# A selective-scan kernel: products written over the drive, six drive buffers, all state copies on ScalarE, and unit 12 of first passes on GpSimd

## The chip, the cores and the metric

The kernel runs on one core of one Trainium2 chip. A core has five engines that each work through their own queue in order: TensorE (PE), VectorE (DVE), ScalarE (ACT), GpSimd (POOL) and SyncE (SP, which issues the DMAs here). TensorE writes PSUM; the other memory is SBUF. The metric is the time of one launch on the device in microseconds (us); lower is better.

## The reference

Two layers run on an input of 8 images of 64 channels and 128x128 pixels in float32. The first makes nine weights per pixel with a small convolution and a softmax, and filters each channel with them. The second is a block around a bidirectional state-space model ("Mamba"), with a convolution, a gated branch and a feed-forward net behind it. What matters here is the selective scan, which runs for each image, for two layers and in two directions over the 16,384 pixels as a sequence:

```python
def selective_scan(u, dt, A, Bm, Cm, D, z):
    dt = jax.nn.softplus(dt)
    dA = jnp.exp(jnp.einsum('bdl,dn->bldn', dt, A))
    dBu = jnp.einsum('bdl,bnl,bdl->bldn', dt, Bm, u)
    ...
    _, hs = jax.lax.associative_scan(comb, (dA, dBu), axis=1)
    y = jnp.einsum('bldn,bnl->bdl', hs, Cm) + D[None, :, None] * u
    return y * jax.nn.silu(z)
```

With 128 channels d and 16 states n, each position has 2,048 recurrences h = dA * h + dBu. The kernel calls dA the decay `w`, dBu the drive `bu`, and hs * Cm the product.

## The kernel before, in words

**Chunks and units.** A scan over 16,384 positions is cut into 16 chunks of T = 1024. One image has four scans ("passes") one after the other: layer 0 forward (pass 0) and backward (pass 1), layer 1 backward (pass 2) and forward (pass 3). Passes 0 and 2 are the first of their layer; passes 1 and 3 have `second` set, add the result of the first, and apply the gate and the output projection. So there are 8 x 4 x 16 = 512 chunks. In a chunk the 2,048 recurrences are 16 units u of 128 partitions, and two units make a pair k = u // 2, whose states j and channel group gp the table `PAIRS` gives.

**One unit.** `decay` (L1124, ACT) writes w = exp(dt * A) into one of two PSUM tiles. `drive` (L1116, POOL) writes the drive of a whole pair, 128x2048, into a `bu` tile in SBUF. `scan` (L1142 or L1144 by direction, DVE) runs the recurrence over 1024 positions from the state of the chunk before. `product` multiplies by Cm. It has two forms, and `on_pool(u)` chooses:
- on POOL, units 0, 2, 6, 8, 10 and 14: the scan writes into `hs` in SBUF, POOL copies the last column into `state` (L1161) and multiplies `hs` in place (L1162);
- on DVE, all odd units and units 4 and 12: the scan writes over w in PSUM, DVE multiplies w into `hs` (L1165), and ACT copies the last column into `state` (L1166).

A unit with an even number that falls just behind a GELU of the feed-forward net also goes to DVE. `collect` (L1181, PE) sums a pair's products over the states with matmuls against `sel_y`. The pair tile `hs` has four buffers of 128x2048, and so has `bu`.

**Feeding a chunk.** Two chunks ahead, matmuls and activations make x, dt, B and C for it (with a SiLU at step 11 and a softplus at step 18 of that chunk, each with loads of activation tables). `dtx` (L1072, POOL) multiplies dt by x, `store_du` and its neighbours write to DRAM, and `load_channels` and `load_states` (L1083, L1094) load the tiles `dup`, `dtp`, `bp` and `cp` back, spread over partitions.

**Other work beside the scans.** Per image and 16 times each: `Front` (the first layer and three norms) of the next image, during passes 2 and 3; `Mix` (convolutions and the product with the branch), late in pass 3 and in pass 0 of the next image; `Ffn` (the feed-forward net), in the rest of pass 0 and pass 1. Their matmuls, `tmp` tiles and multiplications run on the same engines. Behind the last scan comes a tail with the last image's feed-forward net.

**What sets the order.** Nothing is reordered by a scheduler. Each operation is put down by `at(time, phase, fn)`, where `time` is a step (one unit is one step, a chunk starts at step b) and `phase` orders the operations within a step: FEED, SCAN, MID, PROD, EXP, DECAY, REST. The queues are filled in that order; within one step and phase, in the order of the calls. For the units of a chunk:

```python
for k in range(U // 2):
    at(b + 2 * k - 5, REST, self.drive, k)
    at(b + 2 * k + 3 + (k % 4 == 0), REST, self.collect, k)
for u in range(U):
    at(b + u - 2, EXP, self.decay, u)
    at(b + u, SCAN, self.scan, u)
    at(b + u + self.on_pool(u), FEED if self.on_pool(u) else PROD, self.product, u)
```

POOL's queue thus alternates: the product of an even unit u at step u + 1, then at the same step the drive of the pair that begins six steps after u. Two steps earlier or later there is another such pair of instructions; `dtx` stands at step 5 of the chunk before its own (b - 11).

Of the kernel before, what the change touches and what calls it, by code (L numbers as in the profile page):

```python
# [8 lines left out]
F32 = mybir.dt.float32  # L9
BF16 = mybir.dt.bfloat16  # L10
AF = mybir.ActivationFunctionType
ALU = mybir.AluOpType
# [3 lines left out]
P = 128  # L16
# [14 lines left out]
T = 1024  # L31
# [3 lines left out]
U = G * G  # L35
PW = W + 2
FEED, SCAN, MID, PROD, EXP, DECAY, REST = range(7)
# [18 lines left out]
def kernel(ctx: ExitStack, tc: tile.TileContext, a: dict, out: bass.AP):  # L56
# [6 lines left out]
    nc = tc.nc  # L63
# [128 lines left out]
    with tc.tile_pool(name="wspill", bufs=1) as fp, tc.tile_pool(name="wprep", bufs=2) as pp, \  # L192
            tc.tile_pool(name="wps", bufs=4, space=PSUM) as pps:
        with tc.manual_schedule():
# [49 lines left out]
            fw = a["L1_conv_ffn_in_w"].rearrange("o c i j -> o (c i j)")  # L244
# [21 lines left out]
            for k in range(9):  # L266
                i, j = divmod(k, 3)
# [130 lines left out]
    def at(time, phase, fn, *args):  # L398
        steps.setdefault((time, phase), []).append((fn, args))
# [386 lines left out]
    class Ffn:  # L786
# [6 lines left out]
        def load(self, h):  # L793
            if not self.alone:
                self.win[h] = window(xn_img, "fw")
            else:
                if h == 0:
                    self.fw = wk.tile([P, 2, T], F32, tag="bu", name="fw", bufs=4)
                self.win[h] = self.fw[:, h, 0 : (ROWS + 2) * PW].rearrange("p (r w) -> p r w", w=PW)
            load_shifted(self.win[h], xn_img, self.c, h)  # L800

# [42 lines left out]
                    )  # L844

        def before_taps_out(self):
            self.pre = wk.tile([P, 2, T], F32, tag="hs", name="f1", bufs=4)
            for i, bank in enumerate(self.banks):
                lo = 3 * PW * (i % 2)
                nc.scalar.copy(self.pre[:, i // 2, lo : lo + 3 * PW], bank[:, 0 : 3 * PW])  # L850
# [107 lines left out]
    class Chunk:  # L958


        def __init__(self, i):
            self.b, self.l, self.d, self.t, self.second = order[i]
            self.i, self.t0 = i, U * i
            self.first = i % NT == 0
            self.pairs = PAIRS[i % 2]
            r, last = self.t0 % IMAGE, self.b == B - 1
            self.beside_front = (
                FRONT_AT - FRONT_STEP <= r < FRONT_AT + NCH * FRONT_STEP + 16 and not last
            ) or self.t0 < FIRST_FRONT_AT + NCH * FRONT_STEP + 16
            self.prev = None  # L970
            self.bus, self.hss, self.ws = {}, {}, {}
            self.dup, self.dtp, self.bp, self.cp, self.yv = {}, {}, {}, {}, {}
            self.norm = Norm()

# [127 lines left out]
        def on_pool(self, u):  # L1102


            if u % 2 or u % 8 == 4 or self.t0 + u - 1 in gelu_times:
                return False
            return True

        def over_pair(self, what, k):
            j = self.pairs[k][0]  # L1110
# [1 line left out]
            return src.rearrange("p (o t) -> p o t", o=1).to_broadcast([P, 2, T])  # L1112

        def drive(self, k):
            bu = wk.tile([P, 2, T], F32, tag="bu", name="bu", bufs=4)
            nc.gpsimd.tensor_tensor(bu, self.dup[self.pairs[k][1]], self.over_pair("bp", k), ALU.mult)  # L1116
            self.bus[k] = bu

# [10 lines left out]
        def scan(self, u):  # L1129
            k, i = divmod(u, 2)  # L1130
            if u == 0:
                if self.first:
                    self.state = wk.tile([P, U], F32, tag="state", name="state")
                    nc.vector.memset(self.state, 0.0)
                else:
                    self.state = self.prev.state
            if i == 0:
                self.hss[k] = wk.tile([P, 2, T], F32, tag="hs", name="hs", bufs=4)
            w, hs, bu, s0 = self.ws.pop(u), self.hss[k][:, i, :], self.bus[k][:, i, :], self.column(u)
            to = hs if self.on_pool(u) else w  # L1140
            if self.d == 0:
                nc.vector.tensor_tensor_scan(to, w, bu, s0, ALU.mult, ALU.add)  # L1142
            else:
                nc.vector.tensor_tensor_scan(to[:, ::-1], w[:, ::-1], bu[:, ::-1], s0, ALU.mult, ALU.add)  # L1144
            if not self.on_pool(u):
                self.ws[u] = w

        def column(self, u):
            (j, gp), i = self.pairs[u // 2], u % 2
# [5 lines left out]

        def product(self, u):
            k, i = divmod(u, 2)
            j, hs = self.pairs[k][0], self.hss[k][:, i, :]
            c = self.cp[j // 2][:, j % 2, :]
            if self.on_pool(u):  # L1160
                nc.gpsimd.tensor_copy(self.column(u), self.last(hs))  # L1161
                nc.gpsimd.tensor_tensor(hs, hs, c, ALU.mult)  # L1162
            else:
                w = self.ws.pop(u)
                nc.vector.tensor_tensor(hs, w, c, ALU.mult)  # L1165
                nc.scalar.copy(self.column(u), self.last(w))  # L1166

        def collect(self, k):

            hs, gp = self.hss.pop(k), self.pairs[k][1]  # L1170
            if k % 4 == 0:
                self.y = py.tile([P, N], F32, tag="y", name="y")
                for h, s in enumerate(halves):
                    nc.tensor.matmul(  # L1174
                        self.y[C * h : C * h + C, :], dskip[:, self.l, self.d, C * gp : C * gp + C], self.xc[:, s],
                        start=True, stop=False,
                    )
            for h, s in enumerate(halves):
# [63 lines left out]
        def plan(self):  # L1242
# [23 lines left out]
            at(b - 16, DECAY, self.bc_out)  # L1266
            at(b - 14, REST, self.store_bc)
            at(b - 13, REST, self.store_dt)
            at(b - 11, FEED, self.dtx)
            at(b - 10, REST, self.store_du)  # L1270
            j0 = self.pairs[0][0] // 2
            at(b - 10, REST, self.load_states, "bp", j0)
            at(b - 8, REST, self.load_channels, "dup", 0)
            at(b - 6, REST, self.load_channels, "dtp", 0)
            at(b - 5, REST, self.load_states, "bp", 1 - j0)
            at(b - 4, REST, self.load_states, "cp", j0)
            at(b - 3, REST, self.load_channels, "dup", 1)
# [85 lines left out]
```

## Time and profile before

Three runs took 28,833.31, 28,854.13 and 28,859.38 us; the median is 28,854.13. The profiled execution took 28,835.68 us, with a span of 28,833.6 us from the first to the last instruction.

| | per chunk, or in all |
|---|---|
| set-up before the first scan, tail behind the last | 481.8 us, 443.1 us |
| decay on ACT, 8,192 instructions | 1,119 ns each |
| scan on DVE, 8,192 | 2,343 ns each |
| product on DVE, 5,232 | 1,222 ns each |
| product on POOL, 2,960 | 2,352 ns each |
| drive on POOL, 4,096 (two units each) | 4,534 ns each |
| dt times x on POOL, 512 | 2,361 ns each |
| state copy on POOL, 2,960; on ACT, 5,232 | 187 ns; 158 ns each |

How to read it: a chunk takes about 54 us in passes 0 to 2 and 57 us in pass 3, as the starts of the scans of unit 0 show. Durations of neighbours on one engine overlap by some tens of ns in these records, so that the distance from start to start of back-to-back instructions is what an instruction really takes of its engine. An idle time is put down to the instruction behind it, with what ended it ("releaser"). The share of a whole run hides that the four passes differ, so passes are looked at one by one below. For image 4 of 0 to 7 they run from 14,465 to 15,329, to 16,190, to 17,051 and to 17,960 us.

### The profile page before, as it was taken

The page shows a single profiled execution, that of the slowest core. Times are in us where ns is not written, and L with a number is a line of the kernel's source. Part 1 is how long each engine was busy: PE and PEld are TensorE (multiplying, and loading weights), DVE is VectorE, ACT ScalarE, POOL GpSimd, SP SyncE. Part 2 cuts the span into 40 slices and gives each one's busy share as a digit, 9 for nine tenths or more (in the row PEclk, how much of TensorE's full clock was granted, in tenths as well). Part 3 has the DMA queues.
Part 4 walks back from the last instruction along what each step waited for, and adds up shares of the span by engine and source line. Part 5 has one row for each costly group of instructions (what it writes and reads, how often), then busy time and mean ns, then how long its engine had stood idle before and what let it go on. Part 6 is the DMA issues. An engine that isn't in the chain of part 4 may idle for free. (4 is left out here: it accounts for less than half of the span.)

```text
span 28833.6 us, 311734 instructions
## 1 busy us (share of the span) xinstructions
PE 22961.3 (80%) x97708; PEld 7243.9 (25%) x97708; DVE 27012.9 (94%) x17438; ACT 18542.2 (64%) x26170; POOL 27201.8 (94%) x11052
## 2 busy tenths in 40 slices
PE   6666888878788787887878788787887878878578
PEld 3111222223222232222322222222222222222123
DVE  5999999999999999999999999999999999999997
ACT  3666666666666666666666666666666666666663
POOL 3999999999999999999999999999999999999993
PEclk7777888988899888998989889898888988889779
DMA  5776777777777678776777767777777777777574
GB/s 133 226 243 219 237 252 241 247 225 240 255 240 247 226 237 259 238 244 226 243 252 242 239 229 245 248 247 234 233 249 240 252 229 235 251 240 250 203 249 140
DMA packets 2592273, 6762.77 MB, mean 235 GB/s; under 512 B 431270, under 2 KB 736822, under 8 KB 2589462
## 3 DMA queue, kind: packets, MB, share of 16 engines
q1 hardware_dynamic: 2590614, 6742.83, 71.8%
q8 instruction: 775, 12.70, 0.2%
q14 instruction: 884, 7.24, 0.1%
HBM read 5509.49 MB, written 1265.19 MB: 235 GB/s over the span
## 5 line engine op out<-in xcount | busy, mean ns | idle before, releaser
L1116 POOL TENSOR_TENSOR bu<-dup,bp 128x2048 f32<-128x2048 f32 x4096 | 18545.3, 4534 | 9.9 <-DMA dup<-du_dram 2.4
L1124 ACT ACTIVATE w<-dtp,a_neg 128x1024 f32<-128x1024 f32 x8192 | 9159.5, 1119 | 1642.2 <-DVE hs L1144 695.4
L1162 POOL TENSOR_TENSOR hs<-hs,cp 128x1024 f32<-128x1024 f32 x2960 | 6963.1, 2352 | 243.3 <-DMA cp<-bc_dram 5.1
L1165 DVE TENSOR_TENSOR hs<-w,cp 128x1024 f32<-128x1024 f32 x5232 | 6391.3, 1222 | 273.1 <-DMA cp<-bc_dram 96.1
L1144 DVE TENSOR_TENSOR_SCAN w<-w,state,bu 128x1024 f32<-128x1024 f32 x2651 | 6212.3, 2343 | 113.9 <-ACT w L1124 85.6
L1142 DVE TENSOR_TENSOR_SCAN w<-w,state,bu 128x1024 f32<-128x1024 f32 x2581 | 6049.4, 2344 | 173.0 <-ACT w L1124 144.4
L1181 PE MATMUL y<-hs,sel_y 128*32 128x512 f32 x32768 | 4983.5, 688 | 694.4 <-POOL hs L1162 693.6
L1166 ACT COPY state<-w 128x1 f32<-128x1 f32 x5232 | 828.2, 158 | 5460.1 <-DVE hs L1165 5401.8
L1142 DVE TENSOR_TENSOR_SCAN hs<-w,state,bu 128x1024 f32<-128x1024 f32 x1515 | 3548.9, 2343 | 173.4 <-ACT state L1166 71.9
L1144 DVE TENSOR_TENSOR_SCAN hs<-w,state,bu 128x1024 f32<-128x1024 f32 x1445 | 3384.8, 2342 | 151.2 <-ACT state L1166 65.9
L991 PE MATMUL xp<-hn,wx 128*128 128x512 f32 x4096 | 2332.5, 698 | 757.3 <-ACT xc L997 320.9
L822 PE MATMUL fp<-fw,bgw 128*128 128x512 f32 (+1 forms) x5760 | 2196.5, 625 | 242.7 <-DMA fw<-xn_dram 230.9
L1174 PE MATMUL y<-xc,dskip 128*64 128x512 f32 x4096 | 1442.1, 790 | 1123.1 <-ACT yv L1198 972.4
L1033 PE MATMUL dp<-xc,wdt 128*128 128x512 f32 x2048 | 1336.5, 739 | 581.5 <-ACT dt L1040 274.3
L1181 PEld LDWEIGHTS y<-hs,sel_y 128*32 128x32 f32 x32768 | 714.7, 115 | 4242.9 <-issue 2328.2
L68 ACT ACT_TABLE_LOAD x1137 | 1458.8, 1283 | 20.8 <-PEq L1352 0.7
L997 ACT ACTIVATE xc<-xp,cbias 128x512 f32<-128x512 f32 x1024 | 697.6, 681 | 1160.2 <-PE xp L991 1157.0
L828 PE MATMUL fp<-fw,bgw 64*128 64x512 f32 (+1 forms) x5760 | 1381.4, 606 | 0.0
L991 PEld LDWEIGHTS xp<-hn,wx 128*128 128x128 f32 x4096 | 795.2, 212 | 2161.9 <-issue 861.6
L595 PE MATMUL acc<-t,ident 128*128 128x512 f32 x2160 | 1330.5, 703 | 0.0
L580 PE MATMUL wb<-wt,sel_k 65*128 65x512 bf16 x1152 | 509.3, 448 | 919.5 <-DVE t L584 810.3
L1072 POOL TENSOR_TENSOR du<-dt,xc 128x1024 f32<-128x1024 f32 x512 | 1208.7, 2361 | 30.1 <-ACT dt L1046 30.1
(211 smaller groups left out, 24922.6 us busy)
## 6 DMA issues: line engine op xcount, KB each, us to landing
bp<-bc_dram SPq DMA_DIRECT2D x4096, 256.0 KB, 4.0
dup<-du_dram SPq DMA_DIRECT2D x4096, 256.0 KB, 5.2
dtp<-dt_dram SPq DMA_DIRECT2D x4096, 256.0 KB, 5.1
cp<-bc_dram SPq DMA_DIRECT2D x4096, 256.0 KB, 4.8
hn<-hn_dram SPq DMA_DIRECT2D x1024, 256.5 KB, 4.4
dt_dram<-dt SPq DMA_DIRECT2D x512, 512.0 KB, 3.0
du_dram<-du SPq DMA_DIRECT2D x512, 512.0 KB, 2.6
yf_dram<-yv SPq DMA_DIRECT2D x512, 256.0 KB, 4.5
```

Source lines behind the costliest of these rows:

```text
L68: nc.scalar.preload_act_table_set("natural_log_exp_and_others")
L822: nc.tensor.matmul(o, wpair[:, i, g, m], self.win[h][:, i : i + ROWS, 0:W], start=(i == 0), stop=False)
L828: nc.tensor.matmul(o, wlast[rows, i, g, m], self.win[h][rows, i : i + ROWS, lo : W + lo], start=False, stop=(i == 2),)
L991: nc.tensor.matmul(self.xp[h], wx[:, self.l, self.d, i, :], self.hn2[:, s.start + 2 * i : s.stop + 2 * i], start=(i == 0), stop=(i == 1),)
L1116: nc.gpsimd.tensor_tensor(bu, self.dup[self.pairs[k][1]], self.over_pair("bp", k), ALU.mult)
L1124: nc.scalar.activation(w, self.dtp[gp][:, i, :], AF.Exp, scale=a_neg[:, self.l, self.d, g, j : j + 1])
L1142: nc.vector.tensor_tensor_scan(to, w, bu, s0, ALU.mult, ALU.add)
L1144: nc.vector.tensor_tensor_scan(to[:, ::-1], w[:, ::-1], bu[:, ::-1], s0, ALU.mult, ALU.add)
L1162: nc.gpsimd.tensor_tensor(hs, hs, c, ALU.mult)
L1165: nc.vector.tensor_tensor(hs, w, c, ALU.mult)
L1174: nc.tensor.matmul(self.y[C * h : C * h + C, :], dskip[:, self.l, self.d, C * gp : C * gp + C], self.xc[:, s], start=True, stop=False,)
L1181: nc.tensor.matmul(self.y[lo : lo + 32, :], sel_y, hs[:, i, s], start=False, stop=(k % 4 == 3))
```

## The change

- A product is written over its unit's half of the drive tile `bu` instead of into `hs`, on POOL and on DVE alike, and `collect` reads `bu`. The drive tile lives until its `collect`, and `bu` has six buffers instead of four. `hs` is now a tile of one unit (128x1024, four buffers), allocated only for units whose product is on POOL. Two tiles of the last image's feed-forward net (`fw`, `f1`) take `bu` buffers.
- `keep` copies the last column into `state` on ACT for every unit. For a unit on DVE it stands where the ACT copy stood; for a unit on POOL it stands in phase EXP of the step behind the unit, after that step's decay. POOL makes no state copies any more.
- `on_pool` keeps unit 4 on DVE and gives unit 12 to POOL in chunks of first passes.
- `drive` is put down one step earlier, and with it `dtx`, `store_du`, the loads of `bp` and the first load of `dup`.

```diff
         def before_taps_out(self):
-            self.pre = wk.tile([P, 2, T], F32, tag="hs", name="f1", bufs=4)
+            self.pre = wk.tile([P, 2, T], F32, tag="bu", name="f1", bufs=6)
...
-            if u % 2 or u % 8 == 4 or self.t0 + u - 1 in gelu_times:
+            if u % 2 or u == 4 or self.t0 + u - 1 in gelu_times:
                 return False
-            return True
+            return u != 12 or not self.second
...
         def drive(self, k):
-            bu = wk.tile([P, 2, T], F32, tag="bu", name="bu", bufs=4)
+            bu = wk.tile([P, 2, T], F32, tag="bu", name="bu", bufs=6)
             nc.gpsimd.tensor_tensor(bu, self.dup[self.pairs[k][1]], self.over_pair("bp", k), ALU.mult)
...
-            if i == 0:
-                self.hss[k] = wk.tile([P, 2, T], F32, tag="hs", name="hs", bufs=4)
-            w, hs, bu, s0 = self.ws.pop(u), self.hss[k][:, i, :], self.bus[k][:, i, :], self.column(u)
-            to = hs if self.on_pool(u) else w
+            w, bu, s0 = self.ws.pop(u), self.bus[k][:, i, :], self.column(u)
+            to = wk.tile([P, T], F32, tag="hs", name="hs", bufs=4) if self.on_pool(u) else w
+            self.hs[u] = to
...
         def product(self, u):
             k, i = divmod(u, 2)
-            j, hs = self.pairs[k][0], self.hss[k][:, i, :]
-            c = self.cp[j // 2][:, j % 2, :]
-            if self.on_pool(u):
-                nc.gpsimd.tensor_copy(self.column(u), self.last(hs))
-                nc.gpsimd.tensor_tensor(hs, hs, c, ALU.mult)
-            else:
-                w = self.ws.pop(u)
-                nc.vector.tensor_tensor(hs, w, c, ALU.mult)
-                nc.scalar.copy(self.column(u), self.last(w))
+            engine = nc.gpsimd if self.on_pool(u) else nc.vector
+            engine.tensor_tensor(
+                self.bus[k][:, i, :], self.hs[u], self.cp[self.pairs[k][0] // 2][:, self.pairs[k][0] % 2, :], ALU.mult
+            )
+
+        def keep(self, u):
+            nc.scalar.copy(self.column(u), self.last(self.hs.pop(u)))
...
-            hs, gp = self.hss.pop(k), self.pairs[k][1]
+            hs, gp = self.bus.pop(k), self.pairs[k][1]
...
-            at(b - 11, FEED, self.dtx)
-            at(b - 10, REST, self.store_du)
+            at(b - 12, FEED, self.dtx)
+            at(b - 11, REST, self.store_du)
             j0 = self.pairs[0][0] // 2
-            at(b - 10, REST, self.load_states, "bp", j0)
-            at(b - 8, REST, self.load_channels, "dup", 0)
+            at(b - 11, REST, self.load_states, "bp", j0)
+            at(b - 9, REST, self.load_channels, "dup", 0)
             at(b - 6, REST, self.load_channels, "dtp", 0)
-            at(b - 5, REST, self.load_states, "bp", 1 - j0)
+            at(b - 6, REST, self.load_states, "bp", 1 - j0)
...
-                at(b + 2 * k - 5, REST, self.drive, k)
+                at(b + 2 * k - 6, REST, self.drive, k)
...
+            for u in range(U):
+                at(b + u + self.on_pool(u), EXP if self.on_pool(u) else PROD, self.keep, u)
```

More of the change, by code (lines that the diff above doesn't have):

```diff
@@ L797, in load @@
                 if h == 0:
-                    self.fw = wk.tile([P, 2, T], F32, tag="bu", name="fw", bufs=4)
+                    self.fw = wk.tile([P, 2, T], F32, tag="bu", name="fw", bufs=6)
                 self.win[h] = self.fw[:, h, 0 : (ROWS + 2) * PW].rearrange("p (r w) -> p r w", w=PW)
@@ L970, in __init__ @@
             self.prev = None
-            self.bus, self.hss, self.ws = {}, {}, {}
+            self.bus, self.hs, self.ws = {}, {}, {}
             self.dup, self.dtp, self.bp, self.cp, self.yv = {}, {}, {}, {}, {}
@@ L1144, in scan @@
                 nc.vector.tensor_tensor_scan(to[:, ::-1], w[:, ::-1], bu[:, ::-1], s0, ALU.mult, ALU.add)
-            if not self.on_pool(u):
-                self.ws[u] = w
         def column(self, u):
```

## The prediction

> **What bounds the kernel now.** I read the page first. In its 40 slices both DVE and POOL are at 9 nearly everywhere, so the whole does not say which of the two it is.
>
> ```profile
> DVE  5999999999999999999999999999999999999997
> POOL 3999999999999999999999999999999999999993
> ```
>
> So I cut one image (image 4) into its four passes, by the starts of the scans of unit 0, and read the busy time of each engine per pass, in the order pass 0, 1, 2, 3.
>
> ```profile
> core 0: us, PE busy (x) PEld busy (x) DVE busy (x) ACT busy (x) POOL busy (x), PEclk, DMA share, GB/s
> 14465.00:15329.00 864.00, 677.53 (x2834) 181.64 (x2832) 803.20 (x460) 551.22 (x747) 856.56 (x345) 0.87 0.76 246
> 15329.00:16190.00 861.00, 761.90 (x3166) 236.23 (x3164) 832.36 (x506) 584.84 (x795) 832.11 (x318) 0.96 0.74 249
> 16190.00:17051.00 861.00, 656.80 (x2750) 204.79 (x2748) 833.33 (x541) 565.07 (x804) 850.31 (x357) 0.83 0.70 227
> 17051.00:17960.00 909.00, 758.30 (x3533) 273.38 (x3531) 869.97 (x610) 614.93 (x922) 856.19 (x360) 0.90 0.74 242
> ```
>
> In pass 0 POOL is busy 856.56 of 864 us and DVE idles 61 us; in pass 2 POOL leaves 10.7 us and DVE 27.7. In passes 1 and 3 POOL leaves 29 and 53 us, DVE 29 and 39. The groups and waits of POOL say what its rest is: first pass 0 (two groups), then the one large wait of passes 1 and 3.
>
> ```profile
> L1162 POOL TENSOR_TENSOR hs<-hs,cp 128x1024 f32<-128x1024 f32 x93 | 218.8, 2352 | 7.4
> L1161 POOL COPY state<-hs 128x1 f32<-128x1 f32 x93 | 17.4, 187 | 0.0
> ...
> POOL state L1161 <- DVE hs L1144: 22.0, 13, 3.6
> ...
> POOL state L1161 <- DVE hs L1142: 24.9, 19, 3.8
> ```
>
> In pass 0 the only idle time of POOL is 7.4 us, the 80 ns between a state copy and its product (93 times). It waits for nobody: **passes 0 and 2 last as long as POOL's queue.** In passes 1 and 3 POOL waits for scans: there DVE sets the pace. What DVE itself waits for there, in pass 1 (first line) and pass 3 (last two):
>
> ```profile
> DVE w L1144 <- ACT w L1124: 9.9, 6, 2.7
> ...
> DVE t L584 <- PE wb L580: 19.2, 12, 3.0
> DVE hs L1142 <- ACT state L1166: 6.3, 10, 0.9
> ```
>
> Decays that come late from ACT, and matmuls of the front; POOL's drives are not among them. Summing the gaps of the whole trace by pass, and following each releaser back along its engine until DVE or a DMA is met, 0.04 us per chunk of DVE's 1.63 us in pass 1, and 0.02 of 2.49 in pass 3, lead through POOL.
>
> **The change part by part.** *The state copies leave POOL.* Durations overlap, so I take distances from start to start. The timeline of POOL in pass 0:
>
> ```profile
> 14599.96 4.54 POOL L1116 TENSOR_TENSOR bu<-dup,bp 128x2048 f32<-128x2048 f32 x1
> 14604.44 0.18 POOL L1161 COPY state<-hs 128x1 f32<-128x1 f32 x1
> 14604.70 2.35 POOL L1162 TENSOR_TENSOR hs<-hs,cp 128x1024 f32<-128x1024 f32 x1
> 14607.01 4.53 POOL L1116 TENSOR_TENSOR bu<-dup,bp 128x2048 f32<-128x2048 f32 x1
> ```
>
> Drive to copy is 4.48 us, copy to product 0.26, product to drive 2.31. Over the trace the medians are 4.474, 0.265 and 2.310, and drive to drive, with no copy between, is 4.494 (551 cases). A copy thus costs 4.474 + 0.265 - 4.494 = 0.245 us. Passes 0 and 2 have 747 + 754 = 1,501 copies (six a chunk, less 21 and 14 that a GELU sends to DVE): 1,501 x 0.245 = **-368 us**. By the busy row alone (187 ns) it would be -281; the 80 ns gap belongs to the copy and goes with it, so I take the spacing and keep both ends. The Trainium skill (Perfetto Trace Analysis, "GPSIMD Engine Instruction") likewise says that a GpSimd span is unreliable and that start-to-start spacing is to be used; here the two readings differ by 87 us, and the trace's own gaps favour the spacing.
>
> *Unit 12 goes to POOL in first passes.* 256 chunks, none of them behind a GELU, each one product more between two drives: 256 x 2.312 (mean from a product's start to the next drive) = **+592 us** on POOL. Writing into `bu` instead of in place makes three separate tiles, as `dt` times x has, which takes the same (2,361 ns, next start after 2.315). DVE loses 256 x 1.222 = 313 us in the passes where it idles anyway: worth nothing, the cover being POOL's full queue. Were POOL not full there, this would be the gain.
>
> So per first-pass chunk POOL gets 2.31 - 1.44 = 0.87 us longer; in all +224 us, with no idle time on POOL to take it.
>
> *In second passes* POOL loses 1,459 x 0.245 = 357 us of work. It was waiting for scans there, so I cost this at nothing; what is late next is the scan, as now. Products end 0.26 us earlier, which PE's `collect` could use: PE waits for POOL's products 0.84 us per chunk in pass 1 and 0.37 in pass 3. If all of that came back to DVE it would be (0.84 + 0.37) x 128 = 155 us; by the followed waits it is 0.06 x 128 = 8. I take 0 and keep -155 as the low end.
>
> *Drives one step earlier, and six buffers.* On POOL's queue the drive of pair m + 3 now stands before the product of unit 2m instead of behind it; `dtx` keeps its place behind the product of unit 2. The new wait is that a drive waits for the `collect` of six drives before. Today a drive starts at least 3.9 us (pass 0) and 3.4 us (pass 2) behind that point, with medians of 16 and 15, and in POOL's order it moves up by one product, 2.6 us at most: no wait. In pass 1 it moves up by as much as a pair's time (6.7 us) and a tenth of the drives have under 3.7, so waits of some 3 us will be seen; queued behind such a drive is the product of the scan just running. POOL's 1.1 us of waiting per chunk and the 1.3 us of copies removed cover these; without that cover they would cost about 0.6 us a chunk, 80 us.
>
> *The earlier DMAs.* `dup` is needed sooner: from the store of `du` to the first drive of the next chunk POOL has 21.06 us of work now and 18.1 then (three drives and three products with copies now, three drives and two products without then). The store, the `bp` load (which waits for drive 5, directly behind `dtx` as before) and the `dup` load on SP keep their spacing. Today `dup` lands 6.9 us (pass 0) and 6.6 us (pass 2) before that drive in the median, 4.2 and 3.2 at the tenth percentile. Taking 2.96 us from each landing that the trace records leaves none short in pass 0 and 0.12 us a chunk in pass 2: **+15 us**; bounds 0 and, with three times that in both passes, 77.
>
> *All copies on ACT.* 2,960 more at 0.159 us and a gap of 0.033, 0.19 us each, 562 us in all on an ACT that idles 17 to 19 us in each chunk, mostly for DVE's products. Two questions. Does such a copy wait? ACT's copies now start when the DVE product ends, not the scan (5,401.8 us of idle time, "ACT state<-w" behind "DVE hs L1165"), though both only read w; if the new ones waited for POOL's product in the same way, ACT would stand still 2 to 10 us after many scans. But w lies in PSUM and `hs` in SBUF. The Trainium skill (PSUM — Partial Sum Buffer, "PSUM bank collisions raise a hardware error") says that two engines may not even both read a bank at once and must be kept apart by semaphores; by that rule only copies from PSUM wait. The trace has no ACT read of `hs`; the scan alone writes it, and the copy needs only that, so I take no wait and keep the other as a rival. Second, where is ACT's own work the path? Behind the SiLU. In pass 1, ACT:
>
> ```profile
> 15534.31 0.16 ACT L1166 COPY state<-w 128x1 f32<-128x1 f32 x1 [0.28 <-DVE hs L1165]
> ...
> 15540.44 1.12 ACT L1124 ACTIVATE w<-dtp,a_neg 128x1024 f32<-128x1024 f32 x1
> ```
>
> and DVE, which waits at unit 14:
>
> ```profile
> 15541.66 2.35 DVE L1144 TENSOR_TENSOR_SCAN hs<-w,state,bu 128x1024 f32<-128x1024 f32 x1 [0.34 <-ACT state L1166]
> ```
>
> From the copy behind product 11 (15534.31) to the end of decay 14 (15541.56) ACT works without a pause, and scan 14 waits 0.34 us for it; over the trace unit 14 costs 0.29 to 0.38 us per second-pass chunk. The copy of unit 10 lands in this stretch, between decay 13 and the table load: 256 x 0.19 = **+49 us** in second passes (in first passes DVE has room). Other late decays (units 10 and 11 of pass 1, 0.70 us a chunk) and front matmuls behind ACT may take another 0.19; I say in one chunk of four, **+12 us**. Ends: 0, and three such places per chunk, 146 us.
>
> *Sum.* -368 + 592 + 0 + 15 + 49 + 12 = +300 us. On the profiled execution's 28,835.7 us that is 29,136; this execution lies 18.4 us below the median of the three runs, so against that median 29,154. Set-up and tail (481.8 and 443.1 us) keep their instructions; the tail's two tiles use a ring of six where they used two of four, after the drives have ended: nothing. I say 29,150.
>
> **The rivals.** *Second passes give part of it back.* PE's waits for POOL shrink and ACT's copies hide: 28,854 + 224 - 155 to 28,854 + 224 - 60, some 28,960. For it: PE does wait for POOL there. Against: the followed waits of DVE hardly touch POOL.
>
> *Faster (the other side).* In passes 1 and 3 the earlier products and drives smooth PE's order so far that late matmuls and decays vanish for DVE. The place is DVE's 1.63 and 2.49 us of idle time per chunk, in all 527 us; the change is faster by over 0.2% (58 us; about what a measurement can tell here from no change) when more than 239 + 58 = 297 us of it go, 1.16 us per chunk. With 400 us it would be 28,854 + 239 - 400 = 28,690. Against: scans and table loads that cause these waits are unchanged, and ACT gets more work. With 181 to 297 us gone it would end as before.
>
> *The change does not do what it says on ACT:* copies of POOL units wait for POOL's products. In first passes products start 7.7 us (pass 0) and 5.2 us (pass 2) behind their scan, ACT stalls, but decays are still a pair ahead of POOL's need; in second passes up to 0.5 us for each of 1,459 units, up to 730 us: 29,300 to 29,880.
>
> **How the numbers follow.** My forecast 0.63, given back 0.16, faster 0.09, even 0.05, copies that wait or other new waits above the range 0.07. Chances: faster 0.09, within 0.2% 0.05, slower 0.86. The range reaches from the low end of the given-back case (28,854 + 224 - 155 = 28,923, of which I leave a little) to the top of the unknown costs (28,854 + 224 + 77 + 146 = 29,301): 28,940 to 29,290, with about 0.2 outside.
>
> **What will show it.** In the profile after: POOL with under 1 us of idle time per chunk in passes 0 and 2, and no rest between drive and product; a chunk of pass 0 at 54.9 us (now 54.0) and of pass 2 at 54.7 (now 53.7); DVE idle in pass 0 near 6 us. In passes 1 and 3 chunks within 0.4 us of now (53.7 and 57.0), POOL waiting longer for scans, scan 14 waiting about 0.5 us. ACT's 8,192 copies at 158 ns, those of `hs` without a wait. I am wrong if chunks of passes 1 and 3 fall by over half a us, if POOL stands idle in passes 0 and 2 (a late `dup`, a late `collect`), or if a product that is not in place runs at another speed.

## The result, and the profile after

The changed kernel takes 29,094.49 us (median of four runs, 29,086.08 to 29,118.30) against 28,856.76 us before in the same session: a ratio of 1.0084, 95% interval 1.0072 to 1.0097. It is slower by 0.84%, as was forecast; the forecast of 29,150 us lies 0.2% above it. In a later session (the last run below) the ratio was 1.0083 (1.0069 to 1.0096). The profiled execution took 29,102.4 us, its span 29,100.6.

In the 40 slices of the page POOL stays full and DVE is no longer so everywhere:

```profile
DVE  5999999999999999999989999899998999999897
POOL 3999999999999999999999999999999999999993
```

Busy time of each engine in the four passes of image 4, in the order pass 0 to 3 (bounds: the scans of unit 0):

```profile
core 0: us, PE busy (x) PEld busy (x) DVE busy (x) ACT busy (x) POOL busy (x), PEclk, DMA share, GB/s
14602.00:15476.00 874.00, 678.88 (x2830) 182.29 (x2830) 785.18 (x444) 557.00 (x836) 874.00 (x266) 0.86 0.76 242
15476.00:16342.00 866.00, 762.70 (x3165) 237.49 (x3162) 832.87 (x509) 592.69 (x881) 819.11 (x233) 0.95 0.74 247
16342.00:17217.00 875.00, 653.80 (x2748) 202.10 (x2748) 815.33 (x526) 569.92 (x896) 869.57 (x278) 0.84 0.71 224
17217.00:18130.00 913.00, 764.62 (x3535) 278.13 (x3534) 869.98 (x610) 623.10 (x1018) 844.68 (x268) 0.90 0.75 242
```

In pass 0 POOL is busy for all of its 874 us, where it had 7.4 us of gaps before; passes 0 and 2 are 10 and 14 us longer than in the kernel before, passes 1 and 3 are 5 and 4 us longer. The groups of POOL in pass 0 show no idle time before any of them, and the timeline shows why POOL is nevertheless later: the copy between drive and product is gone, and there are 109 products where there were 93.

```profile
L1116 POOL TENSOR_TENSOR bu<-dup,bp 128x2048 f32<-128x2048 f32 x127 | 575.3, 4537 | 0.0
L1156 POOL TENSOR_TENSOR bu<-hs,cp 128x1024 f32<-128x1024 f32 x109 | 257.1, 2359 | 0.0
```

```profile
14702.80 4.55 POOL L1116 TENSOR_TENSOR bu<-dup,bp 128x2048 f32<-128x2048 f32 x1
14707.29 2.37 POOL L1156 TENSOR_TENSOR bu<-hs,cp 128x1024 f32<-128x1024 f32 x1
14709.60 4.56 POOL L1116 TENSOR_TENSOR bu<-dup,bp 128x2048 f32<-128x2048 f32 x1
```

From start to start a drive takes 4.49 us and a product 2.31 us, the forecast's spacings. A product into the drive tile runs at the speed of one in place (2,359 ns here, 2,352 before).

In second passes POOL's waits have changed place. POOL's waits of 40 us and more at drives and products, over the whole trace:

```profile
POOL bu L1116 <- PE y L1176: 344.8, 163, 4.8
POOL bu L1116 <- issue: 219.2, 52, 5.8
...
POOL bu L1116 <- DMA bp<-bc_dram: 81.3, 38, 5.1
POOL bu L1116 <- DMA dup<-du_dram: 78.1, 47, 5.1
...
POOL bu L1156 <- DVE hs L1141: 46.2, 38, 6.9
```

Products now hardly wait for scans (46.2 us; the copies ahead of them waited 366.2 us for DVE and PE before). Drives wait, 825 us in all where it was 9.9: 345 us for PE's `collect` of six drives before (L1176), 159 us for late loads of `bp` and `dup`, and 219 us for something that the profile does not show ("issue").

| mean us per chunk, images 1 to 6 | pass 0 | pass 1 | pass 2 | pass 3 |
|---|---|---|---|---|
| before | 54.02 | 53.62 | 53.79 | 56.93 |
| changed | 54.73 | 54.17 | 54.72 | 57.11 |
| changed, DVE idle (before) | 5.63 (3.80) | 2.13 (1.60) | 3.73 (1.72) | 2.75 (2.57) |
| changed, POOL idle (before) | 0.01 (0.47) | 3.04 (1.70) | 0.35 (0.65) | 4.39 (3.37) |

Over all eight images the four passes grew by 88, 33, 117 and 12 us, 249 in all. The other 18 us by which the two spans differ lie ahead of the first scan (481.8 and 499.7 us). They are probably not the change's: in the twelve other profiled executions below that stretch is 489 to 510 us, in those with all steps of the kernel before too; the profile of before had a short one.

### The profile page after: what moved, and what is told of

Read it like the earlier page. It is cut to its first block, busy times and chain, and to the rows that moved or that the text cites. A ratio compares the mean times of both kernels' runs of the same rounds, so it can differ in the third digit from the quotient of the medians.

```text
span 29100.6 us, 311870 instructions
## 1 busy us (share of the span) xinstructions
PE 23093.8 (79%) x97708; PEld 7270.4 (25%) x97708; DVE 26726.4 (92%) x17182; ACT 18756.1 (64%) x29130; POOL 27294.8 (94%) x8348
## 5 line engine op out<-in xcount | busy, mean ns | idle before, releaser
L1156 POOL TENSOR_TENSOR bu<-hs,cp 128x1024 f32<-128x1024 f32 x3216 | 7632.8, 2373 | 46.3 <-DVE hs L1141 46.2
L1156 DVE TENSOR_TENSOR bu<-w,cp 128x1024 f32<-128x1024 f32 x4976 | 6081.7, 1222 | 364.9 <-DMA cp<-bc_dram 193.2
L1176 PE MATMUL y<-bu,sel_y 128*32 128x512 f32 x32768 | 5054.0, 698 | 1357.4 <-POOL bu L1156 1355.3
L1143 DVE TENSOR_TENSOR_SCAN w<-w,state,bu 128x1024 f32<-128x1024 f32 x2523 | 5914.5, 2344 | 203.8 <-ACT w L1124 180.5
L1141 DVE TENSOR_TENSOR_SCAN w<-w,state,bu 128x1024 f32<-128x1024 f32 x2453 | 5751.3, 2345 | 193.0 <-ACT w L1124 168.3
L1141 DVE TENSOR_TENSOR_SCAN hs<-w,state,bu 128x1024 f32<-128x1024 f32 x1643 | 3850.1, 2343 | 292.2 <-ACT state L1161 181.4
L1143 DVE TENSOR_TENSOR_SCAN hs<-w,state,bu 128x1024 f32<-128x1024 f32 x1573 | 3686.2, 2343 | 319.6 <-ACT state L1161 218.1
L991 PE MATMUL xp<-hn,wx 128*128 128x512 f32 x4096 | 2370.0, 708 | 673.9 <-ACT sq L1218 252.3
L1176 PEld LDWEIGHTS y<-bu,sel_y 128*32 128x32 f32 x32768 | 705.1, 115 | 4920.3 <-POOL bu L1156 2323.8
L991 PEld LDWEIGHTS xp<-hn,wx 128*128 128x128 f32 x4096 | 813.3, 216 | 2105.5 <-issue 951.7
```

The source lines that it names most:

```text
L991: nc.tensor.matmul(self.xp[h], wx[:, self.l, self.d, i, :], self.hn2[:, s.start + 2 * i : s.stop + 2 * i], start=(i == 0), stop=(i == 1),)
L1156: engine.tensor_tensor(self.bus[k][:, i, :], self.hs[u], self.cp[self.pairs[k][0] // 2][:, self.pairs[k][0] % 2, :], ALU.mult)
L1176: nc.tensor.matmul(self.y[lo : lo + 32, :], sel_y, hs[:, i, s], start=False, stop=(k % 4 == 3))
```

## The experiments

The theory: passes 0 and 2 last as long as POOL's queue, a product costs POOL 2.31 us and a copy 0.245, and the change puts on more than it takes off. The rival: the new order costs the time (copies on ScalarE, earlier drives, drive tiles that live longer). Every ratio is to the kernel before, on the same chip in the same session (28,877.57, 28,877.37 and 28,878.46 us in the three sessions).

| kernel | us | ratio (95%) |
|---|---|---|
| before + products over the drive | 28,725 | 0.9948 (0.9935 to 0.9960) |
| ... + all copies on ScalarE | 28,692 | 0.9936 (0.9924 to 0.9949) |
| ... + drives and loads a step earlier | 28,748 | 0.9955 (0.9940 to 0.9970) |
| ... + unit 12 of first passes on POOL = the change | 29,109 | 1.0083 (1.0069 to 1.0096) |

This ladder is what the runs below give when they are set in order; the third line is from another session than the others. A step's worth holds for this order: the next runs show that the copies are worth far more once unit 12 is on POOL.

**Unit 12 back on DVE.** The changed kernel with

```diff
-            return u != 12 or not self.second
+            return u != 12
```

> The changed kernel, but unit 12 stays on DVE everywhere. Queue theory (first passes last as long as POOL's queue, and a product costs it 2.31 us): a chunk of pass 0 falls from 54.7 to 52.4 us on POOL; in pass 2 POOL would fall to 52.3, but DVE has 51.0 + 1.2 us of work and 1 to 2 us of waits that do not come from POOL, so 53.2 to 53.7. In all 29,094 - 128 x 2.0 - 128 x 1.2 = about 28,690 us (28,630 to 28,760), 0.3 to 0.8% faster than the kernel before; second passes unchanged at 53.9 and 56.7. Rival (the time comes from the new order: copies on ScalarE, earlier drives, the later end of a drive tile): within 100 us of the changed kernel, 29,000 to 29,190.

Measured 28,747.99 us, ratio 0.9955 (0.9940 to 0.9970): 346 us less than the changed kernel, and faster than the kernel before. By pass the sums fall by 206 (pass 0), 23 and 126 (pass 2) and rise by 8 us in pass 3, so nearly all is in the first passes, as the theory says and the rival does not. Passes 0 and 2 of image 4, where POOL in the changed kernel was busy for 874.00 of 874 and 869.57 of 875 us:

```profile
14430.00:15278.00 848.00, 672.11 (x2840) 180.72 (x2838) 802.73 (x459) 558.26 (x836) 845.38 (x252) 0.88 0.79 252
16144.00:17008.00 864.00, 657.05 (x2748) 204.49 (x2749) 833.35 (x541) 572.63 (x896) 837.47 (x263) 0.83 0.72 227
```

The fall is less than the 410 us expected. A chunk of pass 0 takes 53.03 us, not 52.4: POOL does 128.8 drives in the pass there and 127.2 in the changed kernel, whose POOL lags, ends the pass with drives still owed and does them in pass 1 (129.8 against 127.7). In pass 2 POOL is no longer full (1.50 us of idle time a chunk; DVE has 1.81, and waits there for loads of `cp`, for ScalarE and for matmuls, hardly for POOL).

**Unit 12 on POOL, and nothing else.** The kernel before with

```diff
-            if u % 2 or u % 8 == 4 or self.t0 + u - 1 in gelu_times:
+            if u % 2 or u == 4 or self.t0 + u - 1 in gelu_times:
                 return False
-            return True
+            return u != 12 or not self.second
```

> The kernel before, with only unit 12 of first passes moved to POOL (POOL still makes its state copies). Queue theory: 256 x (2.31 + 0.245) = +654 us, about 29,510 us (29,400 to 29,560), ratio 1.019 to 1.024, all of it in passes 0 and 2, POOL without idle time there. Rival (a product moved off DVE costs little, since DVE gives up 313 us): 28,860 or less.

Measured 29,473.62 us, ratio 1.0208 (1.0191 to 1.0225): +596 us, in the range. By pass +271, +47, +293 and +14 us. The move that takes 1.22 us off DVE and puts 2.56 on POOL costs nearly its full price on POOL (596 of 654 us); DVE's gain shows as idle time (6.88 us a chunk in pass 0, 3.80 before).

**Copies back on POOL.** The changed kernel with

```diff
             engine = nc.gpsimd if self.on_pool(u) else nc.vector
+            if self.on_pool(u):
+                nc.gpsimd.tensor_copy(self.column(u), self.last(self.hs[u]))
...
-            nc.scalar.copy(self.column(u), self.last(self.hs.pop(u)))
+            h = self.hs.pop(u)
+            if not self.on_pool(u):
+                nc.scalar.copy(self.column(u), self.last(h))
```

> The changed kernel with the state copies of POOL's units back on POOL, just ahead of their product. Queue theory: 1,757 copies in first passes at 0.245 us = +430 us, in second passes between -60 (ScalarE relieved) and +60: about 29,500 us (29,420 to 29,600), ratio to the kernel before 1.020 to 1.026. If a copy cost POOL only its busy time (187 ns): +330, 29,420. Rival (copies on ScalarE are what costs): 29,000 or less.

Measured 29,315.34 us, ratio 1.0151 (1.0135 to 1.0166): 221 us more than the changed kernel, half of what the theory said, and less than a copy's busy time alone would give (330). First the timeline of POOL in the kernel before (from the prediction: copy to product 0.26 us), then in this one:

```profile
14706.70 4.54 POOL L1116 TENSOR_TENSOR bu<-dup,bp 128x2048 f32<-128x2048 f32 x1
14711.15 0.21 POOL L1157 COPY state<-hs 128x1 f32<-128x1 f32 x1
14711.29 2.40 POOL L1158 TENSOR_TENSOR bu<-hs,cp 128x1024 f32<-128x1024 f32 x1
```

Copy to product is 0.14 us here (median 0.137, 0.265 before). The product of the kernel before overwrites the tile that the copy reads, and waits for the copy to end: in 2,724 of its 2,960 cases the semaphore that comes last before the product is the copy's, and the product starts 80 ns behind the copy's end. A product that goes elsewhere starts 54 ns before the recorded end of the copy (both medians). So a copy costs POOL 4.471 + 0.137 - 4.487 = 0.12 us, and the in-place product's wait for it another 0.125. 1,757 copies at 0.12 are 211 us; passes 0 and 2 grew by 95 and 110.

**Products over the drive alone.** The kernel above at the steps of the kernel before, with unit 12 on DVE: against the kernel before it has the new place of the products, six drive buffers and scan tiles of one unit, and no other part of the change. Its core:

```diff
-            if self.on_pool(u):
-                nc.gpsimd.tensor_copy(self.column(u), self.last(hs))
-                nc.gpsimd.tensor_tensor(hs, hs, c, ALU.mult)
...
+            if self.on_pool(u):
+                nc.gpsimd.tensor_copy(self.column(u), self.last(self.hs[u]))
+            engine.tensor_tensor(
+                self.bus[k][:, i, :], self.hs[u], self.cp[self.pairs[k][0] // 2][:, self.pairs[k][0] % 2, :], ALU.mult
+            )
```

> The kernel before with one part of the change alone: products are written over the drive (six drive buffers, a scan tile of one unit); POOL keeps its state copies, unit 12 stays on DVE, and all steps are those of before. With copies on POOL beside a product that is not in place, copy to product took 0.137 us instead of 0.265. If half of a copy's 0.245 us was the in-place product's wait for it: 0.125 us for each of 1,501 copies in first passes, less what DVE then holds back in pass 2: 100 to 190 us faster than before, about 28,720, ratio 0.993 to 0.997. If the whole 0.245 us belongs to the copy itself: no change, ratio 0.998 to 1.002.

Measured 28,725.47 us, ratio 0.9948 (0.9935 to 0.9960): 153 us faster. A chunk of pass 0 falls from 54.02 to 53.48 us. The product follows its copy by 0.14 us here too:

```profile
14543.35 0.24 POOL L1157 COPY state<-hs 128x1 f32<-128x1 f32 x1
14543.49 2.41 POOL L1158 TENSOR_TENSOR bu<-hs,cp 128x1024 f32<-128x1024 f32 x1
14545.80 4.60 POOL L1116 TENSOR_TENSOR bu<-dup,bp 128x2048 f32<-128x2048 f32 x1
```

At 0.125 us each, the 747 and 754 copies of passes 0 and 2 make 93 and 94 us, enough for what the passes lose by the profiles (66 and 18 us; in pass 2 POOL is not full any more). What the six buffers and the smaller scan tiles add, and why pass 1 is 33 us shorter as well, was not tested apart.

**And the copies on ScalarE.** The same kernel with

```diff
-            if self.on_pool(u):
-                nc.gpsimd.tensor_copy(self.column(u), self.last(self.hs[u]))
...
+            nc.scalar.copy(self.column(u), self.last(self.hs.pop(u)))
```

> The kernel of the line above with the copies of POOL's units on ScalarE as well (unit 12 on DVE, steps of before). The other half of a copy, 0.12 us, leaves POOL: 0.7 us a chunk in pass 0, less in pass 2, where DVE sets the pace by now: 50 to 100 us faster than the line above, about 28,650, ratio to before 0.990 to 0.994. If ScalarE's copies cost on DVE's path what they save on POOL: as the line above, 0.995.

Measured 28,691.95 us, ratio 0.9936 (0.9924 to 0.9949): another 33 us, less than the 50 expected at least. Pass 0 falls on to 52.95 us, but pass 2 only from 53.75 to 53.59, where POOL by now idles 1.35 us a chunk and DVE 1.55.

The total hides two effects. Passes 0 and 2 fall by 60 and 27 us, and passes 1 and 3 grow by 42 and 22. That is the second passes' cost that the prediction put on ScalarE, about as large as its +61 us, but mostly in another place: scan 14 waits 0.08 us a chunk longer in pass 1 (0.30 to 0.38) and 0.06 in pass 3, while scan 11 in pass 1 waits 0.27 longer (0.52 to 0.79). Decay 11 stands on ScalarE behind an activation that waits for the matmul `xp` (L991), and ScalarE's wait for that matmul grows from 2.40 to 2.71 us a chunk. Why the matmul comes later was not found. With unit 12 on POOL the same move leaves passes 1 and 3 as they were (within 6 us, from the kernel with copies back on POOL to the changed one).

**Drives and loads at the old steps.** The changed kernel with

```diff
-            at(b - 12, FEED, self.dtx)
-            at(b - 11, REST, self.store_du)
+            at(b - 11, FEED, self.dtx)
+            at(b - 10, REST, self.store_du)
...
-                at(b + 2 * k - 6, REST, self.drive, k)
+                at(b + 2 * k - 5, REST, self.drive, k)
```

and the three loads likewise.

> The changed kernel with drives, dt times x, and the loads of bp and dup at the steps of the kernel before; six buffers and all else as changed. If the earlier drives only move POOL's waits from the products to the drives and cost nothing: within 30 us of 29,095. If the drives' waits for the collect of six drives before and for late loads delay products and so PE and DVE in second passes (products start 1 to 3 us later behind their scan there than before): 30 to 60 us faster, about 29,050. If the earlier drives help: slower than 29,130.

Measured 29,048.50 us, ratio 1.0059 (1.0045 to 1.0073), against 1.0084 and 1.0083: the earlier steps cost about 0.24%, 60 to 70 us, if the chips compare. POOL's groups (drive and product) show that its waits are back at the products:

```profile
L1116 POOL TENSOR_TENSOR bu<-dup,bp 128x2048 f32<-128x2048 f32 x4096 | 18599.5, 4545 | 28.7 <-DMA x_dram<-in_x 6.8 <-DMA dup<-du_dram 5.9 <-DMA bp<-bc_dram 5.5
L1156 POOL TENSOR_TENSOR bu<-hs,cp 128x1024 f32<-128x1024 f32 x3216 | 7606.3, 2365 | 671.8 <-DVE hs L1141 318.0 <-DVE hs L1143 253.4 <-DMA dup<-du_dram 74.4
```

The size is near what was expected, but the place of the gain is not the one that the expectation named: passes 0 and 2 are 25 and 29 us shorter, pass 1 is 7 shorter and pass 3 is 10 longer. In pass 0 POOL does one drive fewer (126.0, with the earlier steps 127.2; products 108.0 and 108.3). In pass 2 the drives are equal (127.0) and the products 109.0 and 109.8. My reading for pass 0 is that with earlier drives POOL does one more drive of the next pass inside the full one; that was not tested by itself, and for pass 2 the cause stays open. Of the rival's parts this is the one that shows in the changed kernel: about a quarter of its loss.

**Later and doubled copies on ScalarE.** First the copies of POOL's units one step later, then each of them twice:

```diff
-                at(b + u + self.on_pool(u), EXP if self.on_pool(u) else PROD, self.keep, u)
+                at(b + u + 2 * self.on_pool(u), EXP if self.on_pool(u) else PROD, self.keep, u)
```

> The changed kernel with the state copies of POOL's units two steps behind the unit instead of one, so that the copy of unit 10 stands behind the SiLU's table loads on ScalarE and not ahead of them. If that copy lengthens the stretch that scan 14 waits for, as predicted: scan 14 waits 0.1 to 0.2 us less per chunk of a second pass, 256 x 0.13 to 0.19 = 33 to 49 us less, about 29,055 us beside 29,095 for the changed kernel. If the copies on ScalarE cost nothing: no difference, 29,095.

```diff
-            nc.scalar.copy(self.column(u), self.last(self.hs.pop(u)))
+            for _ in range(1 + self.on_pool(u)):
+                nc.scalar.copy(self.column(u), self.last(self.hs[u]))
+            self.hs.pop(u)
```

> The changed kernel with each state copy of a unit on POOL made twice on ScalarE: 3,216 copies more, 0.2 us each, 640 us of ScalarE. If ScalarE is the path only behind the SiLU of second passes: +49 us, up to 75, about 29,155. If ScalarE were the path in more places (three a chunk, first passes too): 29,250 to 29,400. If it is nowhere the path: 29,095.

Measured 29,070.27 us, ratio 1.0067 (1.0054 to 1.0079), and 29,078.61 us, 1.0072 (1.0059 to 1.0085). At unit 14 the copies do what was said: the scan waits 0.29 and 0.38 us per chunk (passes 1 and 3) before, 0.43 and 0.46 with the change, 0.34 and 0.38 with later copies, 0.62 and 0.60 with doubled ones. But the passes do not follow: with doubled copies pass 3 takes 57.02 us a chunk and with the change 57.11, pass 1 53.93 and 54.17. What DVE waits longer there it waits less elsewhere: in pass 1 scan 11 waits 0.48 us a chunk with doubled copies and 0.76 with the change, in pass 3 DVE waits 0.93 and 1.16 us for the matmul `wb`. By the ratios the kernel with later copies is 46 to 49 us below the changed one, which is what was expected if the copies lengthen scan 14's stretch, but its passes 1 and 3 fall by 10 us each only, and doubled copies, which should then have cost 49 us, come out below the changed kernel too. So 615 us more of copies on ScalarE cost the changed kernel nothing that these runs can tell. That does not cancel the 64 us of second passes in the run before: what moving the copies costs there changes with the kernel around it and is not settled. The group of the copies from `hs` in the changed kernel also stands without idle time, so none of them waits for POOL's product.

```profile
L1161 ACT COPY state<-w 128x1 f32<-128x1 f32 x4976 | 784.8, 158 | 4983.3 <-DVE bu L1156 4920.1 <-DVE state L1134 40.2
L1161 ACT COPY state<-hs 128x1 f32<-128x1 f32 x3216 | 571.2, 178 | 0.0
```

**Unit 12 on POOL in second passes.** Here POOL has time and DVE sets the pace:

```diff
-            return u != 12 or not self.second
+            return u != 12 or self.second
```

> The changed kernel with unit 12 on POOL in second passes instead of first ones. Queue theory: first passes as with unit 12 on DVE (-400 us); second passes are set by DVE, which loses 1.2 us of work per chunk, while POOL has 3 to 4.3 us to spare: pass 3 falls by about 1.2 us a chunk, pass 1 by 0.5 (POOL at 51.2 + 2.3 = 53.5 becomes its new bound). In all about 28,470 us (28,380 to 28,580), ratio 0.983 to 0.990. Rival (second passes are set by matmuls and decays that come late, not by DVE's work): second passes unchanged, 28,690.

Measured 28,776.52 us, ratio 0.9967 (0.9955 to 0.9979), no better than with unit 12 on DVE. The rival named second passes that do not change (its number for the whole was 28,690): against unit 12 on DVE pass 1 is 14 us shorter and pass 3 11 us longer. The largest waits of DVE in pass 3 of image 4 say where 1.2 us a chunk went; first the changed kernel, then this one.

```profile
DVE t L584 <- PE wb L580: 18.1, 12, 2.9
DVE hs L1141 <- ACT state L1161: 7.9, 10, 1.3
```

```profile
DVE t L584 <- PE wb L580: 22.3, 12, 3.0
DVE hs L1141 <- ACT state L1161: 21.5, 16, 2.1
```

The second line is scan 14's wait for its decay behind the SiLU. It goes from 7.9 to 21.5 us over 16 chunks. ScalarE needs 7.3 us from the copy of unit 11 to decay 14, and DVE had scan 12, product 12, scan 13 and product 13 to do meanwhile, 7.06 us. Without product 12 it is done 1.1 us earlier, and waits. In second passes unit 12's product was nearly free on DVE.

**Unit 4 instead.** The changed kernel with unit 12 on DVE everywhere and unit 4 on POOL in second passes:

```diff
-            if u % 2 or u == 4 or self.t0 + u - 1 in gelu_times:
+            if u % 2 or u == 12 or self.t0 + u - 1 in gelu_times:
                 return False
-            return u != 12 or not self.second
+            return u != 4 or self.second
```

> The changed kernel with unit 12 on DVE everywhere and unit 4 on POOL in second passes. With unit 12 on POOL there, scan 14 waited 1.36 us a chunk in pass 3 for ScalarE's SiLU stretch instead of 0.46, so that DVE's shorter work was lost again. If the place of the unit is what lost it: unit 4 stands behind the softplus, whose stretch is shorter (about 6.0 us against 5.7 us of DVE work), so pass 3 falls by 0.5 to 1.1 us a chunk and pass 1 by up to 0.4: 28,750 - 60 to 190 = 28,560 to 28,690, ratio to the kernel before 0.989 to 0.994. If second passes do not depend on DVE's work at all: 28,750 to 28,780, ratio 0.996 to 0.997.

Measured 28,676.85 us, ratio 0.9930 (0.9917 to 0.9942). Pass 3 falls to 56.14 us a chunk (57.22 with no such move, 57.05 with unit 12), pass 1 to 53.28. By pass sums that is 101 and 43 us. So second passes do depend on DVE's work, where the stretch of another engine behind the unit leaves room. Not all of it comes through in pass 1: scan 10's wait for its decay grows there from 0.06 to 1.09 us a chunk.

**Both together.** Unit 4 as above, and the drives and loads at the old steps:

> The changed kernel with the drives and loads at the steps of before, unit 12 on DVE everywhere and unit 4 on POOL in second passes. If the steps cost the 30 to 60 us that the run at the old steps showed in first passes, and unit 4 its gain in pass 3: 28,620 to 28,650, ratio 0.990 to 0.993. If the steps cost nothing: 28,680, ratio 0.993.

Measured 28,579.00 us, ratio 0.9897 (0.9883 to 0.9910): faster than both kernels, by 1.0% and about 1.8%, and below the 28,620 that was expected at best. Against the kernel with all copies on ScalarE, measured in the same session, the only difference is unit 4 in second passes, and it is worth 113 us (0.9936 to 0.9897). Its four passes in image 4, in order:

```profile
14363.00:15210.00 847.00, 668.71 (x2844) 181.76 (x2840) 802.84 (x459) 558.08 (x836) 845.18 (x253) 0.88 0.79 253
15210.00:16058.00 848.00, 753.68 (x3154) 237.72 (x3146) 813.68 (x491) 591.51 (x878) 847.58 (x246) 0.96 0.73 250
16058.00:16919.00 861.00, 650.39 (x2753) 202.31 (x2751) 833.07 (x545) 573.06 (x901) 836.51 (x263) 0.83 0.73 228
16919.00:17818.00 899.00, 764.87 (x3517) 278.38 (x3513) 850.45 (x591) 620.92 (x1015) 875.41 (x281) 0.89 0.76 244
```

POOL is full in passes 0 and 1 now; in pass 2 POOL and DVE leave 24 and 28 us, and in pass 3 POOL leaves 24 and DVE 49.

**The changed kernel again,** on the chip of the ladder:

> The changed kernel once more, on the chip of the three lines above, so that its parts are compared on one chip: ratio to before 1.0072 to 1.0097 as first measured. If it is 1.007 or less, the run at the old steps (1.0059) and those with later and doubled copies (1.0067, 1.0072) differ from it by no more than chips do.

Measured 29,109.44 us, ratio 1.0083 (1.0069 to 1.0096), as first measured: the parts can be compared across the sessions within the intervals. Pass sums of the two profiles of this kernel differ by up to 9 us, which says how small a difference between two profiles means something.

## Why the prediction was right, and where it was not

*POOL's queue sets passes 0 and 2.* Right. POOL idles 0.01 and 0.35 us a chunk there, and the two kernels that only move unit 12 put the time where it was said. The forecast's 54.9 and 54.7 us a chunk came out as 54.73 and 54.72, in part by chance: with drives and loads at the old steps they are 54.48 and 54.50, so that some 0.2 us a chunk come from the steps, for which the forecast had only 15 us in all.

*Unit 12, +592 us.* About right as a price on POOL: +596 us with the copies in place, where the full sum would be 654; that 596 is close to 592 is chance. Within the change it is worth 346 to 361 us. Without it POOL is not full in pass 2 any more, and in pass 0 it does 1.6 drives more.

*The copies, -368 us.* The spacing of 0.245 us was right and the busy time wrong, but the name was wrong: half of it (0.125 us) was the in-place product's wait and went with the new place of the products, which I had costed at nothing. Without unit 12 the two are worth 153 and 33 us, 186 and not 368: pass 2 gives only 45 us by the profiles, since POOL is not full there any more, and the second passes take 25 back. So both large terms were too large, by about 180 and 240 us, since each was priced on a POOL that stays the bound, and their sum is nearer the mark than either: +224 forecast, about +175 measured.

*All copies on ScalarE, +49 +12 us.* Not borne out in the changed kernel, and not settled. The stretch behind the SiLU and its scan were named rightly, and the wait grew by 0.08 to 0.13 us (0.19 was forecast), but doubling the copies showed that it does not reach the end: "scan 14's wait adds to DVE's time" does not hold there, since other waits of DVE shrink. Moving the copies alone, with unit 12 on DVE, did lengthen second passes by 64 us, mostly at scan 11, behind a matmul and not behind the copies' own time. That the copies do not wait for POOL's product was right.

*Drives and loads a step earlier, +15 us.* Too small: 55 to 70 us (0.9955 against 0.9936, 1.0083 against 1.0059). I looked for late loads in passes 0 and 2, and found few there; I did not ask how many drives fall into the full passes, which may be where the time went in pass 0. I also expected POOL in second passes to wait longer for scans. It waits at the drives, in pass 3 as in pass 1 (for PE's `collect` 1.4 and 1.3 us a chunk), and its products start later behind their scans (5.0 us in pass 1 and 3.1 in pass 3, before 3.2 and 2.5).

*In second passes nothing is gained.* Right, nothing was gained: +33 and +12 us in the traces. In images 1 to 6 a chunk of pass 1 is 0.55 us longer, more than the 0.4 that the prediction allowed. The second chunk of the pass grows by 3.1 us, which fits drives that the lagging POOL owed from pass 0 (129.8 in the pass, 129.0 before) but was not tested. The ninth, twelfth and fifteenth grow by 1.6 to 2.1 us each, where scan 11 now waits for its decay on ScalarE. The rival with a faster kernel needed 297 us of DVE's waits to go; they grew. The rival in which second passes give part of the time back needed them to shrink, and they did not.

That the time came out near the forecast is partly luck, for misses of opposite sign cancel. Copies and unit 12, with the copies' cost on ScalarE, were forecast at 224 + 61 = 285 us and come to about 175 by the ladder; the earlier steps were forecast at 15 and come to 56. In all that is 231 us (238 in the first session) where 300 was forecast.

Of the Trainium skill's rules, two can be set beside runs. Perfetto Trace Analysis ("GPSIMD Engine Instruction") has GpSimd spans read by the distance of starts: the runs agree, for the same copy is recorded with 187 ns before and 223 ns in the kernel with the products over the drive alone, where it takes POOL less time. GPSIMD Engine Reference ("Engine selection") sends elementwise work on two inputs to VectorE: here that holds for unit 12 in first passes (1.22 us on DVE, 2.31 on POOL), makes no difference for unit 12 in second passes, and does not hold for unit 4 in second passes, where POOL has time to spare and the kernel gains 0.25% and, at the old steps, 0.39%.

## What to carry to other kernels

Read a balanced kernel stage by stage: two engines that are both 94% busy over the run bound different stages, and work moved to the one that is full in that stage costs up to its full price there, however much the other gains (596 of 654 us here). Price each part of a change on the bound that the other parts leave, not all on today's. Before taking work off an engine, ask which other engine's stretch hides behind it: in second passes the product of unit 12 was nearly free on DVE, and that of unit 4 was not.

## What the runs showed that I had not expected

- An in-place product behind a copy of the same tile started 0.265 us behind the copy; written elsewhere, 0.137 us. The kernel with this change of place, six drive buffers and smaller scan tiles, and nothing else, is 0.52% faster.
- The copy of one column on ScalarE took 178 ns from SBUF (`hs`) and 158 ns from PSUM (w), and the one from SBUF had no idle time before it.
- Doubled copies on ScalarE, 615 us more of its time, left the time as it was, while the scans behind the SiLU did wait longer; moving the copies there, with unit 12 on DVE, lengthened second passes by 64 us.
